# A gated recurrence in sub-blocks: gates with features on partitions, and later rounds on part of the nodes

## The chip, the cores and the metric

The kernel runs on one core of a Trainium2 chip, and all data is 32-bit floating point. The metric is the device time of one execution in microseconds (us). Engines are named as in the profile: PE (matmul), PEld (its weight loads), DVE (VectorE), ACT (ScalarE), POOL (GpSimd) and SP (SyncE, which only starts transfers).

## The reference

Four graph layers work on `x` of shape (16, 1024, 256) with a sparse weighted adjacency `adj` of shape (16, 1024, 1024). Each adds its result to `x` after a layer norm and a relu. Layers 0, 1 and 3 are dense products. Layer 2 is a recurrence over the 1024 nodes of each graph, and the change is there:

```python
def step(h, i):
    x = jnp.take(h_e, i, axis=1)
    row = jnp.take(norm_adjT, i, axis=1)
    x_par = jnp.einsum('bj,bjd->bd', row, h)
    iou = x @ W_ioux.T + b_ioux + x_par @ W_iouh.T + b_iouh
    r, z = jnp.split(iou, 2, axis=1)
    r, z = (jax.nn.sigmoid(r), jax.nn.sigmoid(z))
    hc = jnp.tanh(x @ W_coux.T + b_coux + x_par * r @ W_couh.T + b_couh)
    h_new = z * x_par + (1.0 - z) * hc
    h = jax.lax.dynamic_update_slice(h, h_new[:, None, :], (0, i, 0))
    return (h, None)
```

A node takes the weighted sum of its neighbours: the new values of those with a smaller number, the old values of the others. About one pair in 32 of different nodes is connected.

## The kernel before

**Layer 2 in blocks and rounds.** The nodes of each graph are cut into NT = 8 blocks of 128. Within a block the kernel sorts them, so that nodes which depend on each other stand as far apart as can be, and cuts the sorted block into NS = 8 sub-blocks of S = 16. One step of the loop treats sub-block (t, s) of all 16 graphs together, 256 columns of node and graph (two groups g of eight graphs with 128 each). Where no node of a sub-block depends on another of the same sub-block, one round of gates is enough. Where there is a chain of dependent nodes, the round is repeated, each time with the change in h that the round before brought: a chain of k nodes takes k rounds. The number of rounds in the program is fixed by position, and a branch on the chip runs more where the data asks for it:

```python
KS = (1, 1, 1, 1, 1, 2, 2, 4)
```

`orders` works out the sorted positions and, for every (t, s), the longest chain over the 16 graphs. It stores `need - KS[s]` in `more`. After the fixed rounds, `tc.If(n_more[0][s] > 0)` runs `one_more`, and a loop in it runs further ones.

**One round.** `x` (features on partitions) is the neighbours' sum. `round_` adds its products with `wh` to the sums `pr`, `pz` and `pc` in PSUM, which `seed_r` and `seed_zc` have filled with the parts of the gates that depend on the inputs alone (class `Gates`). `pr` has features on partitions; `pz` and `pc` have nodes on partitions. Since the product of z with the neighbours' sum needs both in one layout, `x` is turned by four PE transposes (line 815) between the products for `pr` and `pz`. ACT and DVE then make r and r*x (lines 825 and 826; in later rounds line 828 takes the difference from the round before, `drx`), PE adds the products of r*x to `pc`, and ACT and DVE make tanh and the new h (lines 842 to 844), which has nodes on partitions, as `change` (line 796) and the next sub-block's sum (line 989) need it. A later round gives PE the same amount of work as the first, and `change` besides. `ho` holds the h of the rounds before, and `change` works on the difference `dh`.

**Work that fills the gaps.** PE, DVE, ACT and POOL run in an order that is written out by hand (`tc.manual_schedule`). Between the steps of a round, `fill(weight)` puts in tasks that nothing waits for at once: sums of old values for the next block (`base_tasks`, line 615 and, to turn them, line 629), contributions of the new h to later sub-blocks (`far_tasks`, line 764) and to the next block (`next_block`, line 751; `last_tasks`, line 665). Each takes one of three PSUM buffers `pf`, and their evictions are kept in `late` until `evict()` issues them. At the end of a sub-block stand the gates' input products for the next one (lines 728 and 736; in the branch or in its else arm), then the sum at line 989, with which the next sub-block begins (line 937).

**POOL and the queues.** POOL gathers the rows of the sorted adjacency (`aj`, line 692), spreads them over graphs (`bd`, line 708, for later nodes; `ai`, line 699, for the same sub-block), copies inputs (`hs`, line 719), masks base rows (line 593), and scatters h to memory (`hs_d`, line 982). SP's queue carries the other loads.

Of the kernel before, what the change touches and what calls it, by code (L numbers as in the profile page):

```python
# [11 lines left out]
ALU = mybir.AluOpType  # L12
# [14 lines left out]
KS = (1, 1, 1, 1, 1, 2, 2, 4)  # L27
# [12 lines left out]
def gnn_stack(ctx: ExitStack, tc: tile.TileContext, a: dict, out: bass.AP):  # L40
# [65 lines left out]
    def orders(pool, psum):  # L106
# [50 lines left out]
        def rest():  # L157
# [41 lines left out]
            for s in range(NS):  # L199
                nc.vector.scalar_tensor_tensor(junk, sub, float(s), chain, op0=ALU.is_equal, op1=ALU.mult)  # L200
                nc.vector.tensor_reduce(top[:, s : s + 1], junk, AX.X, ALU.max)
            most = pool.tile([1, NS, NT], F32, name="o_most")
            for s0 in range(0, NS, 4):
                pt = psum.tile([P, 512], F32, name="pt")
                for s in range(4):
                    nc.tensor.transpose(pt[:1, s * P : (s + 1) * P], top[:, s0 + s : s0 + s + 1], ident)
                nc.vector.tensor_reduce(most[:, s0 : s0 + 4].rearrange("o s t -> o (s t)"),
                                        pt[:1].rearrange("o (q b) -> o q b", b=B), AX.X, ALU.max)
            need = pool.tile([1, NS, NT], F32, name="o_need")
            nc.vector.memset(need, 1.0)  # L210
            for k in range(1, S):
                nc.vector.scalar_tensor_tensor(need, most, 2.0 ** k, need, op0=ALU.is_ge, op1=ALU.add)
            for k in range(2):
                left = pool.tile([1, NT, NS], F32, name="o_left")
                for s in range(NS):
                    nc.vector.tensor_scalar(left[:, :, s], need[:, s], float(KS[s] + k), 0.0, op0=ALU.subtract, op1=ALU.max)
                nc.vector.tensor_copy(more[k], left.rearrange("o t s -> o (t s)"))
# [322 lines left out]

    def layer_2(shared, early):
        with ExitStack() as st:
# [9 lines left out]
            br = wp.tile([P, DC], F32, name="br")  # L552
            br2 = wp.tile([P, DC], F32, name="br2")
            with nc.allow_non_contiguous_dma(reason="biases, once"):
                nc.sync.dma_start(br, a["b_ioux"][:D].rearrange("(c p) -> p c", p=P))
                nc.sync.dma_start(br2, a["b_iouh"][:D].rearrange("(c p) -> p c", p=P))
            nc.vector.tensor_add(br, br, br2)
            bzc = wp.tile([P, 2 * D], F32, name="bzc")
            bzc2 = wp.tile([P, 2 * D], F32, name="bzc2")
            for t, io, co in ((bzc, "b_ioux", "b_coux"), (bzc2, "b_iouh", "b_couh")):  # L560
                nc.sync.dma_start(t[:, :D], bcast_row(a[io][D:], D))
                nc.sync.dma_start(t[:, D:], bcast_row(a[co], D))
            nc.vector.tensor_add(bzc, bzc, bzc2)
# [6 lines left out]
            nc.vector.tensor_mul(before, before, own[:, :, None].to_broadcast([P, GB, S]))  # L570

# [111 lines left out]
            class Sub:  # L683
# [18 lines left out]
                def behind(self):  # L702
                    n, j0 = self.n - S, (self.s + 1) * S
                    self.bd = None
                    if n > 0:
                        self.bd = big.tile([P, G2, GB, P], F32, name="bd")
# [5 lines left out]
            class Gates:  # L712

                def __init__(self, he, s):
# [4 lines left out]
                    self.gr = big.tile([P, DC, G2 * GR], F32, name="gr")  # L721
                    self.gz = big.tile([P, G2, 2 * D], F32, name="gz")
                    self.tasks = [lambda k=k: self.z(k) for k in range(G2)] + [lambda k=k: self.r(k) for k in range(DC)]

                def r(self, e):
                    pg = psum.tile([P, 2 * D], F32, name="pf", bufs=3)
                    for c in range(DC):
                        nc.tensor.matmul(pg[:, : G2 * GR], wx[:, c, e * P : (e + 1) * P], self.hs[:, c],
                                         start=c == 0, stop=c == DC - 1)
                    return lambda: nc.scalar.activation(self.gr[:, e], pg[:, : G2 * GR], AF.Identity,  # L730
                                                        bias=br[:, e : e + 1])

                def z(self, g):
                    pg = psum.tile([P, 2 * D], F32, name="pf", bufs=3)
                    for c in range(DC):
                        nc.tensor.matmul(pg, self.hs[:, c, g * GR : (g + 1) * GR], wx[:, c, D:],  # L736
                                         start=c == 0, stop=c == DC - 1)
                    return lambda: nc.vector.tensor_add(self.gz[:, g], pg, bzc)  # L738

                def seed_r(self):  # L740
                    nc.scalar.activation(pr, self.gr, AF.Copy)

                def seed_zc(self):
                    nc.scalar.activation(pc, self.gz[:, :, D:], AF.Copy)
                    nc.vector.tensor_copy(pz, self.gz[:, :, :D])
# [31 lines left out]

            pr = psum.tile([P, DC, G2 * GR], F32, name="pr")
            pz = psum.tile([P, G2, D], F32, name="pz")
            pc = psum.tile([P, G2, D], F32, name="pc")  # L780
# [10 lines left out]
            def change(dh, x, ai, fill):  # L791

                px = psum.tile([P, DC, G2 * GR], F32, name="pa")
                for g in range(G2):
                    for c in range(DC):
                        nc.tensor.matmul(px[:, c, g * GR : (g + 1) * GR], dh[:, g, c * P : (c + 1) * P], ai[:, g],
                                         start=g == 0 and c == 0, stop=True, skip_group_check=True)
                fill()
                dx = work.tile([P, DC, G2 * GR], F32, name="dx", bufs=1)
                nc.vector.tensor_copy(dx[:, 0], px[:, 0])  # L800
                nc.scalar.activation(dx[:, 1], px[:, 1], AF.Copy)
                for c in range(DC):
                    nc.vector.tensor_add(x[:, c], x[:, c], px[:, c])
                return dx

            def round_(dx, x, rx, h, fill, to):


                for e in range(DC):
                    for c in range(DC):  # L810
                        add(pr[:, e], wh[:, c, e * P : (e + 1) * P], dx[:, c])
                xr = psum.tile([P, G2, D], F32, name="pa")
                for g in range(G2):
                    for c in range(DC):
                        nc.tensor.transpose(xr[:, g, c * P : (c + 1) * P], x[:, c, g * GR : (g + 1) * GR], ident)
                for g in range(G2):
                    for c in range(DC):
                        add(pz[:, g], dx[:, c, g * GR : (g + 1) * GR], wh[:, c, D : 2 * D])
                evict()
                r = work.tile([P, DC, G2 * GR], F32, name="r")  # L820
                drx = r
                if rx is not None:
                    drx = work.tile([P, DC, G2 * GR], F32, name="drx", bufs=1)
                for e in range(DC):
                    nc.scalar.activation(r[:, e], pr[:, e], AF.Sigmoid)  # L825
                    nc.vector.tensor_mul(r[:, e], r[:, e], x[:, e])  # L826
                    if rx is not None:
                        nc.vector.tensor_sub(drx[:, e], r[:, e], rx[:, e])
                z = work.tile([P, G2, D], F32, name="z")
                nc.scalar.activation(z, pz, AF.Sigmoid)  # L830
                w = work.tile([P, G2, D], F32, name="w")
                nc.scalar.activation(w, pz, AF.Sigmoid, scale=-1.0)
                for g in range(G2):
                    for c in range(DC):
                        add(pc[:, g], drx[:, c, g * GR : (g + 1) * GR], wh[:, c, 2 * D :])
                nc.vector.tensor_mul(z, z, xr)
                if h is not None:
                    nc.vector.tensor_sub(z, z, h)
                fill()
                hc = work.tile([P, G2, D], F32, name="hc", bufs=1)  # L840
                for g in range(G2):
                    nc.scalar.activation(hc[:, g], pc[:, g], AF.Tanh)
                    nc.vector.tensor_mul(w[:, g], w[:, g], hc[:, g])
                    nc.vector.tensor_add(to[:, g], z[:, g], w[:, g])
# [3 lines left out]
            def one_more(x, rx, h, ho, ai, tasks=()):  # L848
# [6 lines left out]

                fill()
                dh = work.tile([P, G2, D], F32, name="dh", bufs=1)
                for g in range(G2):
                    nc.vector.tensor_sub(dh[:, g], h[:, g], ho[:, g])
                nc.gpsimd.tensor_copy(ho, h)  # L860
                dx = change(dh, x, ai, fill)
                r = round_(dx, x, rx, None, fill, h)
                nc.gpsimd.tensor_copy(rx, r)
# [4 lines left out]
            with tc.manual_schedule(engines={mybir.EngineType.PE, mybir.EngineType.DVE, mybir.EngineType.Activation, mybir.EngineType.Pool}):  # L868
# [7 lines left out]
                for task in gx.tasks:  # L876
                    task()()
                sub.own()
# [7 lines left out]
                for t in range(NT):  # L886
# [10 lines left out]
                    for s in range(NS):  # L897
# [6 lines left out]
                        if s == 0:  # L904
                            gx_next = Gates(he, 1)
                            todo = [(1.72, task) for task in gx_next.tasks[:2]] + [(0.86, task) for task in gx_next.tasks[2:]]
                            todo += share + behind
# [310 lines left out]
```

## Time and profile before

| | us |
|---|---|
| median of 3 runs (lowest, highest) | 4867.45 (4866.39, 4873.52) |
| span of the profiled execution | 4855.7 |
| layers 0 and 1, with the ordering | 0 to 1515 |
| layer 2 | 1515 to 3398 |
| layer 3 | 3398 to 4856 |

A line of the groups reads: line of the kernel, engine, operation, tile written <- tiles read, shape, number of instructions | busy time in us, mean duration in ns | idle time of that engine just before them, and what ended it. A line of the table by stage gives the window, its length, the busy time of PE, PEld, DVE, ACT and POOL with the number of instructions, the granted PE clock, and the share and rate of the DMA engines. A 32-bit product shows as two PE instructions, a transpose as one.

### The profile page before, as it was taken

To read this page: it belongs to the slowest core of one execution; us is meant where nothing else is said; L and a number is where in the kernel's file an instruction comes from. 1 tells how busy PE (TensorE), PEld (TensorE's weight loads), DVE (VectorE), ACT (ScalarE), POOL (GpSimd) and SP (SyncE) were. 2 spreads that over 40 slices of the span, in tenths; PEclk is the share of its full clock that TensorE was granted. 3 is DMA by queue.
4 is the path that set the end of the run, shared out by engine and by line. 5 is a ranking of instruction groups with operands and counts; after the bars stand their busy time and mean duration, and the time that the engine had idled before them with its cause. 6 is when DMAs were issued, how large, how long until landed. Compare 5 with 4: busy or idle time off the path is not lost. (4 is left out here: it accounts for less than half of the span.)

```text
span 4855.7 us, 51055 instructions
## 1 busy us (share of the span) xinstructions
PE 4521.4 (93%) x17679; PEld 2951.8 (61%) x17679; DVE 2381.2 (49%) x6366; ACT 1173.7 (24%) x2388; POOL 1602.6 (33%) x1883
## 2 busy tenths in 40 slices
PE   8897899999997999999999999988899999999999
PEld 4443445555555777777777777766455555555556
DVE  6667854455543454545454545454534344344342
ACT  1211112222212222222222222222223223223232
POOL 3223233343323333323222333232534234243231
PEclk9999999999998999999999999999899999999999
DMA  5333235555536444444443444421422231222100
GB/s 158 113 98 104 88 88 185 193 165 174 186 112 214 135 145 130 152 139 141 127 146 125 138 151 152 139 83 37 160 87 70 78 104 65 89 89 78 70 26 18
DMA packets 530494, 577.04 MB, mean 119 GB/s; under 512 B 41552, under 2 KB 438992, under 8 KB 527824
## 3 DMA queue, kind: packets, MB, share of 16 engines
q1 hardware_dynamic: 499056, 460.79, 30.1%
q0 software_dynamic: 31040, 111.44, 6.4%
q8 instruction: 189, 3.10, 0.3%
q14 instruction: 209, 1.71, 0.1%
HBM read 470.17 MB, written 116.65 MB: 121 GB/s over the span
## 5 line engine op out<-in xcount | busy, mean ns | idle before, releaser
L290 PE MATMUL pa<-at,h 128*128 128x512 f32 x1088 | 490.2, 603 | 32.8 <-DVE ag L295 32.8
L1093 PE MATMUL ph<-ag,w 128*128 128x512 f32 x1024 | 479.1, 611 | 33.9 <-DVE hh L1097 33.8
L1131 PE MATMUL po<-w,hh 128*128 128x256 f32 x2048 | 447.7, 379 | 0.0
L615 PE MATMUL pf<-hb,ab 128*128 128x256 f32 x1568 | 416.9, 385 | 24.3 <-ACT bs L602 18.8
L290 PE MATMUL pa<-at,q 128*128 128x512 f32 x960 | 424.5, 595 | 0.0
L1131 PEld LDWEIGHTS po<-w,hh 128*128 128x128 f32 x2048 | 387.8, 190 | 59.3 <-issue 7.9
L290 PEld LDWEIGHTS pa<-at,h 128*128 128x128 f32 x1088 | 207.6, 194 | 273.9 <-issue 228.1
L1093 PEld LDWEIGHTS ph<-ag,w 128*128 128x128 f32 x1024 | 179.1, 190 | 295.5 <-DVE hh L1097 151.8
L1099 POOL TENSOR_TENSOR ss<-ss,sq 128x512 f32<-128x512 f32 x224 | 302.4, 1350 | 121.8 <-ACT sq L1096 117.4
L615 PEld LDWEIGHTS pf<-hb,ab 128*128 128x128 f32 x1568 | 281.5, 192 | 75.5 <-ACT bs L602 26.1
L982 POOL DMA_INDIRECT hs_d<-h,table x128 | 129.8, 1014 | 589.0 <-DVE gz L738 420.1
L290 PEld LDWEIGHTS pa<-at,q 128*128 128x128 f32 x960 | 178.4, 190 | 215.8 <-issue 212.8
L736 PE MATMUL pf<-wx,hs 128*128 128x512 f32 x512 | 242.0, 613 | 29.2 <-POOL hs L719 21.6
L1097 DVE TENSOR_SCALAR hh<-ph,b 128x512 f32<-128x512 f32 x256 | 190.0, 746 | 154.7 <-ACT sq L1096 120.7
L1078 PE MATMUL pa<-bxt,h 128*128 128x512 f32 x512 | 228.0, 598 | 19.7 <-POOL bxt L1060 19.7
L764 PE MATMUL pf<-bd,h 128*128 128x384 f32 (+5 forms) x768 | 217.7, 371 | 28.6 <-DVE bxt L767 28.6
L826 DVE TENSOR_TENSOR r<-r,x 128x256 f32<-128x256 f32 x230 | 128.4, 581 | 225.5 <-ACT r L825 225.5
L1078 PE MATMUL pa<-at,h 128*128 128x512 f32 x512 | 228.8, 597 | 0.0
L1096 ACT ACTIVATE sq<-ph,b 128x512 f32<-128x512 f32 x224 | 153.5, 685 | 234.2 <-PE ph L1093 189.1
L1123 ACT ACTIVATE hh<-hh,rw 128x512 f32<-128x512 f32 x256 | 168.4, 712 | 138.7 <-DVE hh L1122 136.7
L1134 DVE TENSOR_TENSOR x<-x,po 128x256 f32<-128x256 f32 x120 | 50.5, 420 | 289.0 <-PE po L1131 288.9
L1078 PEld LDWEIGHTS pa<-bxt,h 128*128 128x128 f32 x512 | 97.4, 192 | 136.9 <-issue 115.3
(233 smaller groups left out, 7723.4 us busy)
## 6 DMA issues: line engine op xcount, KB each, us to landing
at<-in_adjT SPq DMA_DIRECT2D x64, 1024.0 KB
ab<-in_adj SPq DMA_DIRECT2D x128, 512.0 KB
bxt<-in_adjT SPq DMA_DIRECT2D x64, 512.0 KB
at<-in_adjT SPq DMA_DIRECT2D x64, 512.0 KB
ad<-in_adj SPq DMA_DIRECT2D x128, 128.0 KB
x_d<-x POOLq DMA_DIRECT2D x16, 1024.0 KB, 5.4
he_d<-h POOLq DMA_DIRECT2D x16, 1024.0 KB, 9.3
heT_d<-hT POOLq DMA_DIRECT2D x16, 1024.0 KB, 4.2
```

What stands on the lines that cost most here:

```text
L290: nc.tensor.matmul(pa, h[:, mt, c * P : (c + 1) * P], at[n0 // 512][:, mt], start=mt == 0, stop=mt == NT - 1)
L615: nc.tensor.matmul(pb, ab[:, jts[k]], hb[:, jts[k]], start=k == 0, stop=k == len(jts) - 1)
L736: nc.tensor.matmul(pg, self.hs[:, c, g * GR : (g + 1) * GR], wx[:, c, D:], start=c == 0, stop=c == DC - 1)
L764: nc.tensor.matmul(pf, h[:, g, c * P : (c + 1) * P], bd[:, g, b4 : b4 + 4, S : S + far], start=True, stop=True)
L982: nc.gpsimd.indirect_dma_start(out=hs_d[t][g][:, :], out_offset=row(1, g, t, s), in_=h[:, g], in_offset=None)
L1078: nc.tensor.matmul(pa, h[b][:, mt, c * P : (c + 1) * P], at[b][n0 // NH][:, mt], start=mt == 0, stop=mt == NT - 1)
L1093: nc.tensor.matmul(ph, w1[:, c, k * P : (k + 1) * P], ag[:, c, n0 : n0 + NH], start=c == 0, stop=c == DC - 1)
L1096: nc.scalar.activation(sq, ph, AF.Square, bias=b1[:, k : k + 1])
L1097: nc.vector.tensor_scalar(hh[:, k], ph, b1[:, k : k + 1], None, op0=ALU.add)
L1099: nc.gpsimd.tensor_tensor(ss, ss, sq, ALU.add)
L1123: nc.scalar.activation(hh[:, k], hh[:, k], AF.Silu, scale=rw[:, k : k + 1])
L1131: nc.tensor.matmul(po, hh[:, c, k * P : (k + 1) * P], w2[:, c], start=c == 0, stop=c == HC - 1)
```

## The change

All gates of layer 2 now have features on partitions; h comes out as `hT` with features on partitions and is turned to nodes on partitions by four PE transposes and two ACT copies (`turned`). The transposes of `x` are gone. Rounds after the first work only on the nodes from a position `cut` on: `CUTS` gives it for each later round. KS of the last position goes from 4 to 5. `orders` looks also for chains among nodes ahead of a cut, and where it finds one sends all of the sub-block's later rounds to the branch. `one_more` no longer works with differences: it seeds the three sums again from the inputs and does a full round. POOL prepares `bd` of the next sub-block one sub-block ahead (three buffers), behind the first h of the current one: the small copies into `tick` hold it back until then. The gates' biases are loaded with features on partitions.

```diff
-KS = (1, 1, 1, 1, 1, 2, 2, 4)
+KS = (1, 1, 1, 1, 1, 2, 2, 5)
+CUTS = {5: (8,), 6: (8,), 7: (4, 4, 12, 12)}
...
+            for s, cuts in CUTS.items():
+                for k, cut in enumerate(cuts):
+                    if cut in cuts[:k]:
+                        continue
+                    nc.vector.tensor_scalar(junk, pos, float(s * S + cut), None, op0=ALU.is_lt)
+                    nc.vector.scalar_tensor_tensor(junk, sub, float(s), junk, op0=ALU.is_equal, op1=ALU.mult)
+                    nc.vector.scalar_tensor_tensor(junk, chain, 2.0 ** (k + 1), junk, op0=ALU.is_ge, op1=ALU.mult)
+                    nc.vector.tensor_reduce(found, junk, AX.X, ALU.max)
+                    nc.vector.tensor_tensor(early[:, s : s + 1], early[:, s : s + 1], found, ALU.max)
...
+            for s in range(NS):
+                nc.vector.scalar_tensor_tensor(need[:, s], again[:, s], float(KS[s] - 1), need[:, s], op0=ALU.mult, op1=ALU.add)
...
-                        self.bd = big.tile([P, G2, GB, P], F32, name="bd")
+                        self.bd = big.tile([P, G2, GB, P], F32, name="bd", bufs=3)
...
-                    self.tasks = [lambda k=k: self.z(k) for k in range(G2)] + [lambda k=k: self.r(k) for k in range(DC)]
+                    self.g = big.tile([P, 3, DC, G2 * GR], F32, name="gates")
+                    self.tasks = [lambda q=q: self.gate(q) for q in (1, 2, 0)]
...
-                xr = psum.tile([P, G2, D], F32, name="pa")
-                for g in range(G2):
-                    for c in range(DC):
-                        nc.tensor.transpose(xr[:, g, c * P : (c + 1) * P], x[:, c, g * GR : (g + 1) * GR], ident)
-                for g in range(G2):
-                    for c in range(DC):
-                        add(pz[:, g], dx[:, c, g * GR : (g + 1) * GR], wh[:, c, D : 2 * D])
...
+                for q, pg in ((0, pr), (1, pz)):
+                    for e in range(DC):
+                        for c in range(DC):
+                            add(from_(pg[:, e], cut), wh[:, c, q * D + e * P : q * D + (e + 1) * P], dx[:, c])
...
+            def turned(hT, fill, to):
+
+                ph = psum.tile([P, DC, G2, P], F32, name="pa")
+                for e in range(DC):
+                    for g in range(G2):
+                        nc.tensor.transpose(ph[:, e, g], hT[:, e, g * GR : (g + 1) * GR], ident)
+                fill()
+                for e in range(DC):
+                    nc.scalar.activation(to[:, :, e * P : (e + 1) * P], ph[:, e], AF.Copy)
+                evict()
...
-                dx = change(dh, x, ai, fill)
-                r = round_(dx, x, rx, None, fill, h)
-                nc.gpsimd.tensor_copy(rx, r)
+                px = x_change(h, ai, 0)
+                fill()
+                gx.seed_r()
+                gx.seed_zc()
...
+                round_(xm, xm, None, 0, None, fill, hT)
+                turned(hT, fill, h)
...
-                        sub.behind()
...
+                        rx = round_(x, x, None, 0, None, rest_if(False, 1.3), hT)
...
+                            nc.gpsimd.tensor_copy(tick, rx[:, DC - 1, :1])
...
+                        turned(hT, rest_if(K == 1, 0.5), dh)
                         if sub_next:
+                            nc.gpsimd.tensor_copy(tick, dh[:, G2 - 1, D - 1 :])
+                            sub_next.behind()
                             sub_next.own()
...
+                            if last:
+                                rx = round_(dx, xs, rx, cut, None, rest_if(False, 1.3), hT)
+                                turned(hT, rest_if(True, 0.5), h)
+                            else:
+                                rx = round_(dx, xs, rx, cut, hT, rest_if(False, 1.3), changes[cut])
                                 dh = work.tile([P, G2, D], F32, name="dh", bufs=1)
+                                turned(changes[cut], rest_if(False, 0.5), dh)
+                                nc.gpsimd.tensor_tensor(from_(hT, cut), from_(hT, cut), from_(changes[cut], cut), ALU.add)
```

## The prediction

> **What bounds the kernel now.** I read the page first (busy shares), then the table by stage, then sub-blocks of the recurrence one by one, then the groups by shape, then the order of time inside one sub-block.
>
> ```profile
> PE 4521.4 (93%) x17679; PEld 2951.8 (61%) x17679; DVE 2381.2 (49%) x6366; ACT 1173.7 (24%) x2388; POOL 1602.6 (33%) x1883
> ```
> The table by stage, layer 2 alone (window, us, then busy time of PE, weight loads, DVE, ACT, POOL):
> ```profile
> 1515.00:3398.00 1883.00, 1753.82 (x8538) 1400.47 (x8536) 922.87 (x2165) 486.06 (x1134) 578.84 (x818) 0.99 0.41 131
> ```
> PE is busy 93% of it: only 129 us can be won by shorter waits, the rest by less PE work. Six windows, each one sub-block (t,s) = (2,2), (3,2), (2,5), (2,7), (3,7), (7,7):
>
> ```profile
> 2033.00:2059.00 26.00, 24.29 (x110) 18.19 (x110) 10.77 (x25) 5.68 (x14) 9.43 (x13) 1.00 0.48 149
> 2261.00:2294.50 33.50, 31.11 (x146) 23.99 (x146) 16.40 (x40) 8.93 (x22) 9.25 (x13) 1.00 0.36 113
> 2109.00:2137.00 28.00, 27.67 (x146) 23.07 (x145) 14.38 (x37) 8.21 (x20) 7.82 (x13) 1.00 0.37 120
> 2166.00:2213.30 47.30, 46.05 (x234) 38.72 (x232) 25.37 (x61) 14.65 (x37) 10.54 (x17) 1.00 0.41 132
> 2419.80:2475.60 55.80, 53.17 (x271) 44.42 (x269) 31.11 (x75) 17.76 (x45) 9.88 (x17) 1.00 0.33 106
> 3343.00:3398.00 55.00, 40.72 (x172) 32.94 (x172) 26.82 (x62) 14.27 (x36) 4.74 (x5) 0.87 0.16 54
> ```
> A trip through the branch costs 33.5 - 26.0 = 7.5 us at s=2 and 55.8 - 47.3 = 8.5 us at s=7. PE idles 1.7 us in a one-round sub-block, 0.3 at s=5, 1.3 at s=7. The groups:
>
> ```profile
> L863 POOL COPY r<-r 128x512 f32<-128x512 f32 x11 | 6.7, 613 | 81.4 <-DVE drx L828 81.4
> L826 DVE TENSOR_TENSOR r<-r,x 128x256 f32<-128x256 f32 x230 | 128.4, 581 | 225.5 <-ACT r L825 225.5
> L843 DVE TENSOR_TENSOR w<-w,hc 128x256 f32<-128x256 f32 x230 | 97.0, 422 | 144.9 <-ACT hc L842 144.2
> L783 PE MATMUL pc<-wh,r 128*128 128x256 f32 x512 | 125.3, 385 | 12.3 <-DVE r L826 12.2
> L764 PE MATMUL pf<-bd,h 128*128 128x192 f32 x128 | 32.1, 339 | 6.0 <-DVE bxt L767 6.0
> L764 PE MATMUL pf<-bd,h 128*128 128x128 f32 x128 | 24.7, 280 | 0.0
> L764 PE MATMUL pf<-bd,h 128*128 128x64 f32 x128 | 22.2, 260 | 5.3 <-DVE bxt L767 5.3
> ```
> L863 stands in the branch alone: eleven trips. A product shows as two instructions; L764 runs in pairs, so the pitch is a pair's busy time less one duration: 2x0.251-0.339 = 0.163 us at 192 columns, 0.106 at 128, 0.087 at 64. And the end of a round at s=7:
>
> ```profile
> 2435.17 1.89 PE L783 MATMUL pc<-wh,drx 128*128 128x256 f32 x8
> ...
> 2437.12 1.89 PE L615 MATMUL pf<-hb,ab 128*128 128x256 f32 x8
> 2437.16 0.66 ACT L842 ACTIVATE hc<-pc 128x256 f32<-128x256 f32 x2 [0.70 <-PE pc L783]
> ...
> 2438.83 0.42 DVE L844 TENSOR_TENSOR dh<-z,w 128x256 f32<-128x256 f32 x1
> 2438.85 1.18 PE L796 MATMUL pa<-ai,dh 128*128 128x128 f32 x8
> ```
> Eight instructions of 256 columns take 1.89, four (L615 elsewhere) 1.03: pitch 0.215. The new h is complete 2.2 us after pc; queued base work (L615) covers that.
>
> **What the skill says.** TensorE: Matmul & The Clock Gate, § Architectural detail: ACT and DVE are strict FIFO, PE only draws weight loads ahead; so a transpose waiting for h stops all PE work behind it, as L764 behind an unread pf buffer does here. Same page, § LDWEIGHTS: 128 weight columns take P/1.2 = 107 ns, a floor for narrow matmuls; the trace is a little below (0.087 at 64 columns), and I use the trace. Same page, Part 1: an idle stretch of about 3.4 us halves the PE clock; the (7,7) window, at 0.87, agrees. SBUF — State Buffer, § Who interferes with whom: a DVE instruction with two SBUF inputs waits for a GpSimd instruction that reads SBUF. Agrees: r*x and w*hc have one shape, but r*x ran while POOL built bd (581 against 422 ns).
>
> **The change part by part.** Sums are against the profiled span, 4855.7; the three timed runs have median 4867.45, and I carry the difference over.
>
> *Trips.* The inputs are fixed, and the ordering (bins, positions, chains) can be stepped through on them: chains exceed KS in 11 sub-blocks, as L863 shows: five at s=7 (t=0,3,4,6,7), all of five links, six at s=2 to 4. With KS[7]=5 the five go; no node ahead of a cut has a long chain, so `again` is zero everywhere. Left: six trips.
>
> *s=5 and s=6.* Round two has 128 columns: 24x(0.215-0.106) = 2.6 us of PE less. But its r chain becomes the limit: 0.2 from pr's last column, ACT 0.27 (by the line through L825, 381 ns at 256, and L830, 597 at 512), DVE 2x0.28 (L767 at 128 columns: 281 ns), 1.03 us in all against 8x0.106 = 0.85 of pz; with the second half of drx behind it, some 0.6 us of wait. The turn of h after round one (four transposes 0.43, 0.2, two ACT copies 0.66) adds 1.3 us behind a fill of about 10% and 0.5 to 1 us shows. Net -1.1 (bounds -2.3, +1) x14, -1 for t=7: -16 us.
>
> *s=7.* Before: three later rounds at 24x0.215+0.43+0.86 (change) = 6.45. After: two at 24x0.163+1.29 = 5.2, two at 24x0.087+1.29 = 3.4: PE -2.2. Added: four turns in fills of 4%, 0.5 each; r chains 0.8; and bd of the next block (L708 at 1024: 2x1.91 us on POOL, moved behind the first dh) collides with r*x of round two, 1.0. Net about +2 (bounds -1, +6) x8 = +16; five trips x-8.5 = -42.5. Sum -26.
>
> *One-round sub-blocks.* PE work is the same: gates 24x0.215 = 5.2 against 8x0.43+8x0.215 = 5.2; four transposes move from x to h. Post-pc fill is 46% of the todo work, 4 to 6 us for t<7, over the 2.2 us until h; behind them on PE stand the last fill and the gates (5.2), under which ACT's copies to h lie; behind those on ACT stands only a bs of the base, which the next fill needs. So nothing, bounds -0.3 and +0.8 each, -12 to +32 over 40. At t=7 fill is 1 to 2 us: +2. In POOL's queue `tick` holds bd and ai (up to 4.7 us) until h; behind them stand only the scatter to hs_d, masks and the next gather, used a sub-block later. With bd off the r chain, the 12.2 us before pc shrink: -8 (bounds 0, -12).
>
> *The six trips left.* Without h-ho, drx and the POOL copies; with three seeds (ACT 0.60+0.58, DVE 0.69, under the first gate task, 1.7) and a turn: PE 0.86+5.2+0.43 = 6.5 as before. Nothing; bounds -1, +2 each.
>
> *Start and ordering.* bd goes ahead of ai and the second hs on POOL: its 3.8 us delay the first gates (today 1513.8): +4. Biases come as single elements on SP's queue ahead of he: 0 to +3, in that. `orders` gains 4x5 DVE operations of about 0.3 us and eight PE transposes queued behind them: +3 (0 to 7).
>
> Sum: -16 -26 +2 -8 +4 +3 = -41 us. 4867 - 41 = 4826.
>
> **The rivals.** *The turn shows everywhere (slower).* If hT comes late (ACT's bs copies stand ahead of hc when a turn of base falls in that fill, up to 0.9 us) PE stops at the transposes in all 64 sub-blocks and six trips. At 1.1 us each, +77: 4903. It decides above 0.6 us each. For it: 1.3 us of new latency in each round, no fill at t=7; against it: 4 to 6 us of fill in 35 of 64. *More gain.* The 1.7 us of one-round idle come mostly from L764 waiting for a pf buffer whose eviction DVE has behind h; splitting the fill evicts earlier. Half of it back over 40: -28 more, 4798. *A wash.* Narrow rounds are all latency: s=5 and 6 gain nothing (+16), s=7 costs +4 (+16): 4858. *It doesn't do what it says*, cuts failing into the branch: the inputs exclude it.
>
> **How the numbers follow.** About 0.2% (10 us) can be told from no change. Forecast 55% (4800 to 4855), more gain 18%, a wash 11%, turn shows 16%. The wash lies at the edge and is split, 3% faster and 8% same: faster 0.76, same 0.08, slower 0.16. The range 4790 to 4882 takes in more gain, the wash, and the low end of the slower case.
>
> **What would show it.** Right: no L863-like trips at s=7 (about 49 us in each block), s=5 near 27, one-round windows near 26 and 24, r*x near 422 ns. Wrong: PE idle before the transposes of hT over 1 us a sub-block, s=7 without a trip above 53, or layers 0 and 1 longer by over 10.

## The result, and the profile after

The changed kernel is slower: 4911.49 us, median of 4 runs (4903.53 to 4916.15), against 4868.41 for the kernel before; the ratio is 1.0085, 95% interval 1.0068 to 1.0103. I had forecast 4826. The profiled spans are 4908.1 and 4855.7, so 52.4 us are to be explained in them; that is 9 more than the 43 of the medians, because the profiled execution of the kernel before was some 10 us shorter than its median.

Less PE work, and still a longer span. The page's busy shares of the changed kernel:

```profile
PE 4510.6 (92%) x18307; PEld 3022.5 (62%) x18307; DVE 2290.3 (47%) x6408; ACT 1213.9 (25%) x2651; POOL 1586.5 (32%) x1947
```

The table by stage for layer 2, which lasts 1928.9 us now (window, us, then busy time of PE, weight loads, DVE, ACT, POOL, granted PE clock, DMA share, GB/s):

```profile
1522.20:3451.10 1928.90, 1737.22 (x9152) 1467.28 (x9152) 822.31 (x2175) 524.45 (x1397) 557.99 (x884) 0.98 0.42 127
```

PE's busy time fell from 1754 to 1737 us, but its idle time rose from 129 to 192. The layer starts 7.5 us later (1522.2 against 1514.7). The same six windows as in the prediction, sub-blocks (2,2), (3,2), (2,5), (2,7), (3,7) and (7,7):

```profile
2053.70:2081.00 27.30, 24.60 (x118) 19.65 (x117) 10.78 (x25) 6.23 (x15) 8.91 (x15) 1.00 0.44 131
2294.60:2330.40 35.80, 32.81 (x153) 26.36 (x153) 15.19 (x35) 9.97 (x25) 8.90 (x15) 0.95 0.32 95
2134.80:2163.00 28.20, 26.23 (x155) 22.84 (x154) 11.98 (x36) 8.36 (x23) 7.60 (x15) 1.00 0.41 118
2190.60:2243.90 53.30, 48.47 (x278) 40.69 (x276) 23.84 (x74) 16.60 (x52) 12.80 (x19) 1.00 0.37 112
2454.00:2508.30 54.30, 48.75 (x278) 40.77 (x276) 24.12 (x73) 17.20 (x53) 13.51 (x20) 1.00 0.36 110
3397.50:3451.10 53.60, 38.90 (x172) 33.56 (x172) 19.25 (x61) 13.04 (x44) 4.48 (x7) 0.72 0.15 46
```

The trips at s=7 are gone: (2,7) and (3,7) are alike. But a one-round sub-block went from 26.0 to 27.3 us, and a block at s=7 without a trip from 47.3 to 53.3. Added up over t from the start of each sub-block in the trace, after less before, us:

| s=0 | s=1 | s=2 | s=3 | s=4 | s=5 | s=6 | s=7 | start |
|---|---|---|---|---|---|---|---|---|
| +20 | -2 | +14 | +6 | +17 | -1 | -13 | +5 | +7.5 |

The sub-blocks s=0 to 4, where I had expected next to nothing, cost 55 us, more than the whole difference. The groups of PE in layer 2 of the changed kernel, with shapes kept apart, name the waits:

```profile
L749 PE MATMUL pf<-hs,wx 128*128 128x256 f32 x1512 | 349.2, 387 | 15.8 <-POOL hs L740 15.8
L1037 PE MATMUL pa<-bd,h 128*128 128x128 f32 x448 | 64.6, 287 | 52.7 <-ACT gates L757 41.6 <-ACTq L1016 5.9 <-DVEq L1014 4.6
L870 PE MATMUL pa<-ident,hT 128*128 128x128 f32 x376 | 61.7, 279 | 14.4 <-DVE hT L861 13.3 <-DVE w L860 1.1
L827 PE MATMUL pa<-ai,dh 128*128 128x32 f32 x128 | 18.9, 294 | 8.1 <-ACT dh L873 8.1
L870 PE MATMUL pa<-ident,change 128*128 128x128 f32 x96 | 18.5, 291 | 9.2 <-DVE change L861 8.2 <-DVE w L860 1.0
L827 PE MATMUL pa<-ai,dh 128*128 128x96 f32 x128 | 18.3, 286 | 7.1 <-ACT dh L873 5.8 <-issue 1.3
L771 PE MATMUL pnx<-bd,h 128*128 128x128 f32 x448 | 60.1, 277 | 6.0 <-ACT gates L757 5.2 <-issue 0.8
```

In the kernel before, the sum (L989) and the products that read hs (L736) read:

```profile
L989 PE MATMUL pa<-bd,h 128*128 128x128 f32 x448 | 60.1, 277 | 9.4 <-DVEq L966 4.7 <-DVEq L968 4.1 <-PEq L966 0.7
L736 PE MATMUL pf<-wx,hs 128*128 128x512 f32 x502 | 233.6, 606 | 15.5 <-POOL hs L719 7.9 <-DVE bxt L767 3.7 <-ACT bs L602 3.6
```

L1037 is the sum of h with which a sub-block hands over to the next (L989 before). PE waits 41.6 us there, and the releaser is not the turned h (L873) but L757, ACT's eviction of the r gates: 0.99 us at the end of each of the 42 sub-blocks s=1 to 6 without a trip. L771 is the sum's counterpart at the end of s=7. The end of sub-block (2,4) in the changed kernel, in order of time:

```profile
2125.73 0.66 ACT L873 ACTIVATE h<-pa 128x256 f32<-128x256 f32 x2 [6.74 <-PE pa L870]
...
2127.29 5.34 PE L749 MATMUL pf<-hs,wx 128*128 128x256 f32 x24
...
2132.73 0.84 ACT L757 ACTIVATE gates<-pf,bias 128x256 f32<-128x256 f32 x2 [4.70 <-PE pf L749]
...
2133.63 1.16 PE L1037 MATMUL pa<-bd,h 128*128 128x128 f32 x8 [0.99 <-ACT gates L757]
2133.85 1.04 POOL L1030 DMA_INDIRECT hs_d<-h,table  x1 [4.75 <-ACT gates L757]
```

h is complete at 2126.4 us, 7 us before the sum that reads it. Between them lies the branch, with the gates (L749) in both its arms. Behind the branch the sum and POOL's scatter of h start only when ACT has done the last thing it does in the arm. It is h that they wait for and not the PSUM bank `pa`, which ACT reads last and into which L1037 writes: the scatter does not touch the bank, and L771 writes to `pnx`, which ACT never reads, yet both wait for L757. The same place in the kernel before, where DVE wrote h:

```profile
2106.04 1.89 PE L728 MATMUL pf<-hs,wx 128*128 128x256 f32 x8
...
2106.24 0.69 DVE L738 TENSOR_TENSOR gz<-pf,bzc 128x512 f32<-128x512 f32 x1 [0.95 <-PE pf L736]
2107.17 0.47 ACT L730 ACTIVATE gr<-pf,br 128x256 f32<-128x256 f32 x1 [3.82 <-PE pf L728]
2107.22 0.97 POOL L982 DMA_INDIRECT hs_d<-h,table  x1 [0.61 <-DVE gz L738]
...
2107.77 1.05 PE L989 MATMUL pa<-bd,h 128*128 128x128 f32 x8
2107.97 0.48 ACT L730 ACTIVATE gr<-pf,br 128x256 f32<-128x256 f32 x1 [0.33 <-PE pf L728]
```

There too this scatter, the second of two, starts behind DVE's last eviction of the arm (L738, ending 2106.93). That end lies ahead of the end of PE's last gate products, so PE does not wait; ACT's last eviction begins at 2107.97, after the sum has begun. Here h is written in two halves, one for each group of graphs, and the first scatter, which reads the first half, started at 2105.57, behind DVE's last eviction but one. It looks as if the readers wait for a count of the writer's instructions; no run shows more of the reason.

At s=0 the wait goes through POOL. The scatter (L1030) is late, so is the copy of hs behind it in POOL's queue, and the gates of (t,1), which read hs, are the first work of s=0. Sub-block (2,0) in the order of time, changed kernel:

```profile
1999.83 0.84 ACT L757 ACTIVATE gates<-pf,bias 128x256 f32<-128x256 f32 x2 [5.18 <-PE pf L749]
...
2000.94 1.04 POOL L1030 DMA_INDIRECT hs_d<-h,table  x1 [15.12 <-ACT gates L757]
...
2003.28 0.75 POOL L740 COPY hs<-he 128x256 f32<-128x256 f32 x2
...
2003.74 7.13 PE L749 MATMUL pf<-hs,wx 128*128 128x256 f32 x24 [2.23 <-POOL hs L740]
```

The 24 instructions of these products take 7.13 us, against 5.34 in (2,4): the idle 2.23 us are followed by a stretch at half clock. The table by stage, for 6 us that begin within these products, shows a granted clock of 0.81 with PE busy throughout:

```profile
2006.00:2012.00 6.00, 6.00 (x24) 5.09 (x23) 1.38 (x2) 0.84 (x2) 1.02 (x3) 0.81 1.12 384
```

This wait for hs is not all new. The kernel before has 7.9 us of it in the line of L736 above, 1.9 to 2.4 us at s=0 behind each of the four blocks that end with a trip, and under 0.1 behind the other three; the changed kernel has it behind all seven.

The theory of the experiments: **the arm's end**. h counts as written, behind the branch, only when the engine that wrote it has reached the end of its work in the arm. The rival: **the turn itself**, the longer way from pc to h (transposes, copies), costs time in each sub-block, as my slower rival had it. A second question is why a block at s=7 takes 53 us and not 49.

### The profile page after: what moved, and what is told of

Same layout as the page of the kernel before. It is cut to its first block, busy times and chain, and to the rows that moved or that the text cites. A ratio compares the mean times of both kernels' runs of the same rounds, so it can differ in the third digit from the quotient of the medians.

```text
span 4908.1 us, 52731 instructions
## 1 busy us (share of the span) xinstructions
PE 4510.6 (92%) x18307; PEld 3022.5 (62%) x18307; DVE 2290.3 (47%) x6408; ACT 1213.9 (25%) x2651; POOL 1586.5 (32%) x1947
## 5 line engine op out<-in xcount | busy, mean ns | idle before, releaser
L637 PE MATMUL pf<-hb,ab 128*128 128x256 f32 x1568 | 435.1, 390 | 22.1 <-ACT bs L624 18.8
L749 PE MATMUL pf<-hs,wx 128*128 128x256 f32 x1536 | 358.3, 390 | 30.0 <-POOL hs L740 30.0
L749 PEld LDWEIGHTS pf<-hs,wx 128*128 128x128 f32 x1536 | 297.5, 196 | 74.8 <-POOL hs L740 33.1
L1030 POOL DMA_INDIRECT hs_d<-h,table x128 | 129.4, 1011 | 490.6 <-ACT gates L757 386.9
L754 DVE TENSOR_TENSOR gates<-pf,bias 128x512 f32<-128x512 f32 x128 | 88.4, 691 | 231.6 <-PE pf L749 231.6
```

Of the source, the lines that this page charges most:

```text
L637: nc.tensor.matmul(pb, ab[:, jts[k]], hb[:, jts[k]], start=k == 0, stop=k == len(jts) - 1)
L749: nc.tensor.matmul(pg[:, e], wx[:, c, q * D + e * P : q * D + (e + 1) * P], self.hs[:, c], start=c == 0, stop=c == DC - 1)
L1030: nc.gpsimd.indirect_dma_start(out=hs_d[t][g][:, :], out_offset=row(1, g, t, s), in_=h[:, g], in_offset=None)
```

## The experiments

All times are medians; ratios are to the kernel before, whose median beside these runs is 4869. Labels name the edit.

**Which engine writes h** (e1_turn_on_dve):

```diff
-                    nc.scalar.activation(to[:, :, e * P : (e + 1) * P], ph[:, e], AF.Copy)
+                    nc.vector.tensor_copy(to[:, :, e * P : (e + 1) * P], ph[:, e])
```

> The changed kernel with the two copies that end a turn of h on DVE instead of ACT; the gates' order stays. Theory (the arms' end): since ACT writes h, the sum that opens the next sub-block waits, behind the branch, for the last thing that ACT does in the arm, the eviction of the r gates, which comes after the last gate product. With DVE writing h it waits for DVE, whose last work in the arm lies two thirds of the gates earlier. So the 0.99 us before the near sum (sub-blocks 1 to 6) and the 0.75 us at s=7 go, and at s=0 the scatter and the hs copies come about 1 us earlier: 50 to 62 us less, 4849 to 4861. Rival (the turn itself is too long): two copies of 0.42 on DVE are no shorter than two of 0.38 on ACT, so the time stays at 4911 within 10. Rival (PE clock): nothing changes.

Measured: 4855.63, ratio 0.9969 (0.9961 to 0.9977). This is the range of the theory. The turn is no shorter, its copies have only changed engine (420 ns each on DVE, 382 on ACT), and 56 us are gone.

**In which order the arm's work comes** (e2_r_gates_first): the r gates, which ACT evicts, first instead of last.

```diff
-                    self.tasks = [lambda q=q: self.gate(q) for q in (1, 2, 0)]
+                    self.tasks = [lambda q=q: self.gate(q) for q in (0, 1, 2)]
```

> The changed kernel with the gates in the order r, z, c: ACT's eviction comes first in the arm, DVE's last. Theory (the arms' end) in its narrow form, ACT alone: the wait before the near sum goes, 4850 to 4861. In its wide form (behind the branch PE waits for the last work of every engine that wrote h or touched the bank in either arm, DVE too since one_more reads the bank there): the wait changes hands, DVE's eviction of 0.69 us against ACT's 0.84, and the time falls by 10 or less, 4900 to 4911. Rival (the turn is too long): no change.

Measured: 4833.97, ratio 0.9925 (0.9908 to 0.9942), 77 us less than the changed kernel; the turn is untouched. More than expected, because s=0 gained too (29 us over its seven later sub-blocks, while s=1 to s=7 together gained 46). The groups of layer 2, this run:

```profile
L749 PE MATMUL pf<-hs,wx 128*128 128x256 f32 x1512 | 341.5, 381 | 2.9 <-POOL hs L740 2.2 <-issue 0.7
L1037 PE MATMUL pa<-bd,h 128*128 128x128 f32 x448 | 63.2, 284 | 15.4 <-DVEq L1016 5.6 <-DVEq L1014 4.8 <-ACTq L1014 0.7
```

No wait for ACT's gates is left before the sum, and none for DVE's has come in its place, as the wide form would have it; for hs it is 2.2 instead of 15.8 us. Sub-block (2,0) in the order of time:

```profile
1985.19 0.84 ACT L757 ACTIVATE gates<-pf,bias 128x256 f32<-128x256 f32 x2 [1.73 <-PE pf L749]
...
1986.31 1.04 POOL L1030 DMA_INDIRECT hs_d<-h,table  x1 [11.67 <-ACT gates L757]
...
1988.64 0.75 POOL L740 COPY hs<-he 128x256 f32<-128x256 f32 x2
...
1989.28 5.35 PE L749 MATMUL pf<-hs,wx 128*128 128x256 f32 x24
```

The scatter still waits for L757, but L757 now comes early; the 24 instructions take 5.35 us. Layer 2 fell from 1928.9 to 1853.6 us: PE's idle time by 55 and its busy time, for the same number of instructions, by 20. Most of the 20 is the half clock: by the trace's record of the granted clock PE was busy at half speed for 88 us of layer 2 in the changed kernel and for 54 in this run (36 in the kernel before), and half of that difference is 17 us.

**The same in the kernel before** (b1_z_gates_last): there DVE writes h and evicts the z and candidate gates, so these are put last.

```diff
-                    self.tasks = [lambda k=k: self.z(k) for k in range(G2)] + [lambda k=k: self.r(k) for k in range(DC)]
+                    self.tasks = [lambda k=k: self.r(k) for k in range(DC)] + [lambda k=k: self.z(k) for k in range(G2)]
...
-                            todo = [(1.72, task) for task in gx_next.tasks[:2]] + [(0.86, task) for task in gx_next.tasks[2:]]
+                            todo = [(0.86, task) for task in gx_next.tasks[:2]] + [(1.72, task) for task in gx_next.tasks[2:]]
```

> The kernel before with the gates in the order r, then z and c, nothing else. There DVE writes h, and DVE evicts z and c. Theory (the arms' end): the near sum now waits for DVE's eviction after the last gate product, about 0.9 us in sub-blocks 1 to 7 and the scatter before s=0 with it: 45 to 60 us more, 4913 to 4928, the loss of the change without any of the change. Rival (turn, narrow rounds or clock cause the loss): the order of the gates is indifferent, 4868 within 10.

Measured: 4924.5, ratio 1.0121 (1.0103 to 1.0139). An order of gates alone, with no turn of h anywhere, costs the kernel before 55 us, as the theory said, and PE's idle time ahead of its sum (9.4 us before) has the name that the theory gives:

```profile
L989 PE MATMUL pa<-bd,h 128*128 128x128 f32 x448 | 71.2, 287 | 34.6 <-DVE gz L738 23.7 <-DVEq L968 5.6 <-DVEq L966 4.7
```

**Both edits at once** (e6_r_first_turn_on_dve): r gates first as in e2, copies on DVE as in e1. Each alone is a gain; by the theory they undo each other, since DVE then evicts last and writes h.

> The changed kernel with the r gates first and, besides, the copies of the turned h on DVE. Both edits alone made it faster (by 56 and by 77 us). Arms' end: with r first, DVE evicts the gates last (c), so h written by DVE ties the next sub-block's sum to the end of the arm again: slower than with r first alone by 15 to 30 us, 4849 to 4865, with a wait for DVE's gates before the sum. Rival (each edit is a gain of its own, by less ACT work or an earlier turn): 4775 to 4825, both gains together.

Measured: 4904.27, ratio 1.0072 (1.0053 to 1.009). Seventy us slower than e2, and beyond the range that I had given: as at s=0 in the changed kernel, the wait for hs came back too, which I had not counted. The groups of layer 2:

```profile
L749 PE MATMUL pf<-hs,wx 128*128 128x256 f32 x1512 | 350.0, 388 | 18.0 <-POOL hs L740 18.0
L1037 PE MATMUL pa<-bd,h 128*128 128x128 f32 x448 | 63.3, 284 | 47.9 <-DVE gates L754 36.8 <-DVEq L1016 5.6 <-DVEq L1014 4.8
```

The four kernels make a square, in which each edit helps or hurts according to the other:

| us | ACT evicts last (r gates last) | DVE evicts last (r gates first) |
|---|---|---|
| ACT writes h | 4911.5 | 4834.0 |
| DVE writes h | 4855.6 | 4904.3 |

As the cause of the loss the turn falls with this: it is in all four. So does a gain of its own for either edit, by less work on ACT for instance.

**Rounds at full width** (e3_full_rounds): the changed kernel with all later rounds over all nodes.

```diff
-CUTS = {5: (8,), 6: (8,), 7: (4, 4, 12, 12)}
+CUTS = {5: (0,), 6: (0,), 7: (0, 0, 0, 0)}
...
-            changes = {cut: wp.tile([P, DC, G2 * GR], F32, name=f"change{cut}") for cut in (4, 12)}
+            changes = {cut: wp.tile([P, DC, G2 * GR], F32, name=f"change{cut}") for cut in (0,)}
```

> The changed kernel with every cut at 0: later rounds take all 256 columns. Theory (narrow rounds gain, as the forecast had it): s=5 and s=6 lose 1.1 to 2.6 us each (18 to 40 in all) and s=7 about 6 to 8 us a block (48 to 64): 4977 to 5015. Rival (narrow rounds are all latency, and cause the loss): within 10 of 4911, or less.

Measured: 5004.9, ratio 1.0277 (1.0258 to 1.0296), in the range of the theory: narrowing alone is worth 93 us.

**The kernel before with five rounds** (b2_five_rounds):

```diff
-KS = (1, 1, 1, 1, 1, 2, 2, 4)
+KS = (1, 1, 1, 1, 1, 2, 2, 5)
```

> The kernel before with five rounds at s=7 instead of four and nothing else: the five trips at s=7 go, eight full-width rounds come. My prediction's step (a trip at s=7 costs 8.5 us): a full round costs about the same as a trip, so +8 x 8.5 - 5 x 8.5 = +25 us: 4894 (4884 to 4904). Rival (the branch itself, its jump and its empty fills, is the dear part, a round inside the block is cheaper by over 3 us): 4870 or less.

Measured: 4877.51, ratio 1.0017 (1.0008 to 1.0026): 8 us and not 25, between the two ranges. The block (2,7) takes 54.6 us, so the fifth round costs 7.3 us where a trip costs 8.5, and 8 x 7.3 - 5 x 8.5 = +16, as in the traces (s=7 in sum 438 against 422). The trace of the kernel before is of an execution some 10 us shorter than its median, so 16 there and 8 in the medians do not contradict each other. These two runs split the price of a block at s=7. The block (2,7) in the table by stage, first the kernel before with five rounds, then the changed kernel with full rounds:

```profile
2167.30:2221.90 54.60, 53.88 (x271) 44.26 (x269) 31.02 (x73) 17.80 (x44) 11.34 (x18) 1.00 0.36 116
```
```profile
2214.30:2276.20 61.90, 56.24 (x278) 44.61 (x276) 31.33 (x74) 20.43 (x52) 14.21 (x19) 1.00 0.31 97
```

Rounds and width are equal; layout, turn and POOL's order differ. They cost 7.3 us a block, of which 2.4 are PE's busy time and 4.9 its idle time (0.9 of it the arm's end, at L771). No run tells layout, turn and POOL's order apart. Narrowing takes 8.6 us a block off (61.9 to 53.3).

**Four rounds at s=7, r gates first** (e5_r_first_four_rounds), e2 with:

```diff
-KS = (1, 1, 1, 1, 1, 2, 2, 5)
-CUTS = {5: (8,), 6: (8,), 7: (4, 4, 12, 12)}
+KS = (1, 1, 1, 1, 1, 2, 2, 4)
+CUTS = {5: (8,), 6: (8,), 7: (4, 4, 12)}
```

> The changed kernel with the r gates first (4834 us) and with four rounds at s=7 instead of five, so that the five trips at s=7 come back: what did the fifth round cost, and what did the trips? Reading of the traces: the fifth round takes 8.5 us in each of eight blocks (a no-trip block 53 -> about 44.5: -68 us), a trip with a turn 8.5 to 9.5 us (+45): about 4811 us (4800 to 4825). My prediction's own figures (a round of 64 columns for about 5 us, a trip for 8.5): -40 + 42, no difference, 4836. If a trip with three seeds and a turn costs over 13 us, this run is slower than 4834.

Measured: 4818.54, ratio 0.989 (0.987 to 0.991): the fastest kernel of this study, 93 us below the changed one and about 50 below the one before. Its blocks (2,7), without a trip, and (3,7), with one:

```profile
2159.00:2204.80 45.80, 43.97 (x248) 37.60 (x247) 23.44 (x60) 15.11 (x45) 13.43 (x20) 1.00 0.45 140
2403.80:2457.70 53.90, 50.72 (x280) 42.64 (x279) 27.77 (x70) 19.14 (x55) 12.61 (x19) 1.00 0.37 114
```

A trip costs 8.1 us. The fifth round costs 53.0 (e2) - 45.8 = 7.2 us, although it has a quarter of the columns and the full-width one of b2 costs 7.3. So -7.2 x 8 + 8.1 x 5 = -17, and -15 was measured.

**The start of the layer** (e7_four_own_first), e5 with ai and the masks ahead of bd at the start:

```diff
-                sub.behind()
                 sub.own()
+                sub.behind()
```

> As the run with the r gates first and four rounds, but at the start of the layer the near matrices are built behind ai and the first masks, as in the kernel before: only the layer's first 8 us are touched. My prediction put +4 on this at the start (3.8 us of POOL ahead of the second sub-block's hs): so 2 to 4 us less than that run; nothing in between the rest.

Measured: 4824.84 (4817.88 to 4829.77), ratio 0.9909 (0.9887 to 0.993), against e5's 4812.53 to 4825.2: the spreads overlap, so nothing can be told. In the traces the layer's first sub-block takes 17.2 us in this run and 18.5 in e5, but it takes 17.0 in the changed kernel, which starts as e5 does. So the 2 to 4 us that I had said are not shown.

## Why the prediction was wrong

**The step that failed** is that of the one-round sub-blocks: behind the transposes stand "the last fill and the gates (5.2), under which ACT's copies to h lie", "So nothing, bounds -0.3 and +0.8 each". The copies do lie there: the transposes of hT wait 14.4 us in all, but in one-round sub-blocks only in the six with a trip, 0.3 us each, and h is ready 7 us early. But I asked only when h is ready. The reader stands behind a branch, and there it is released by the last work of h's writer in the arm. The change moved the writer from DVE to ACT, whose last work hangs on PE's last gate product. Price: 0.99 us of PE at the end of each sub-block s=1 to 6 without a trip (41.6 us), 5.2 at s=7, and for hs at s=0 about half of 15.8, since the kernel before had 7.9. The forecast also had no term for the clock, though it had named the half clock: PE's busy time at half speed rose from 36 to 88 us, which costs half of the difference, 26. Layer 2 as a whole grew by 46 us: 62 more of idle time and 26 of half clock, less 43 of PE work that is gone. e2 takes 77 us back, more than was lost, in part since it also removes waits for hs that the kernel before has. I had named the scatter in POOL's queue and called it "used a sub-block later"; I had not asked what it waits for now, nor that hs for the next gates stands behind it at s=0.

**The slower rival** came near in number (4903) by luck: it put the wait before the transposes, at 1.1 us in each sub-block, and one-round sub-blocks without a trip have none there. e2 keeps the turn and is 0.75% faster than the kernel before. Only at s=7 does the turn show, as follows.

**s=7** was mis-sized. Said: about 49 us in each block, in sum -26 with the five trips. Measured: 53.0, and +5 in sum. That the trips go was right, and their price too (8.5; e5 has 8.1). Wrong was the narrow round. A round over 64 columns in (2,7) of the changed kernel, pr to pr (the order of time):

```profile
2222.91 1.00 PE L802 MATMUL pr<-dx,wh 128*128 128x64 f32 x8
...
2223.75 1.06 PE L802 MATMUL pz<-dx,wh 128*128 128x64 f32 x8
...
2225.86 1.95 PE L637 MATMUL pf<-hb,ab 128*128 128x256 f32 x8
...
2229.05 1.08 PE L827 MATMUL pa<-ai,dh 128*128 128x32 f32 x8 [0.38 <-ACT dh L873]
...
2230.65 1.00 PE L802 MATMUL pr<-dx,wh 128*128 128x64 f32 x8
```

From the start of pr to that of pz eight instructions take 0.84 us, a pitch of 0.105 and not the 0.087 that I read out of pairs; at s=5, with 128 columns, the same eight take 0.89. The Trainium skill, TensorE: Matmul & The Clock Gate, § LDWEIGHTS, gives 107 ns for 128 weight columns; the trace agrees here, and I had set it aside. From start to start of its pieces the round takes PE 0.84 (pr), 0.99 (pz), 1.12 (pc, which meets the r chain), 0.44 (turn) and 0.91 (change), 4.3 us where I had put 3.4; a round of 192 columns, in the same way (the second of (2,7) in e5), 5.8 where I had put 5.2. So PE's own time rose, from 46.05 to 48.47 us in (2,7), where I had said 2.2 less. Its idle time rose by 3.6, from 1.25 to 4.83, near the 3.8 that turns, r chains and bd had been given (2 + 0.8 + 1.0), but only by luck, since the parts differ. In (2,7) of the changed kernel PE waits 1.5 us at the transposes and 1.7 at the products of dh, 3.2 for four turns where I had put 2; 0.5 at the products of drx, where r chains and bd had 1.8; and 0.9 at L771, the arm's end, which I had not counted. Waits of 1.2 us of the kernel before are nearly gone. Of the 4 us by which a block is longer than said, some 3 are thus the narrow rounds' own PE time, mis-sized by 0.6 us in two rounds and 0.9 in two; the rest is not told apart.

**s=5 and s=6**: -14 against -16 said, which is luck: it holds 0.99 us of arm's end in each, and without it (e2: 215 and 211 us, against 224 and 232) it is -30. So the r chains and turns cost less than I had put, and the gain lay nearer the bound of -2.3.

**Held**: r*x takes 422 ns in the first round, as I had expected with bd moved off it. PE waits 4.3 instead of 12.3 us for it:

```profile
L844 DVE TENSOR_TENSOR r<-r,x 128x256 f32<-128x256 f32 x128 | 48.8, 422 | 139.5 <-ACT r L843 112.1 <-issue 27.4
```

This is the -8 of the sum, and it agrees again with the Trainium skill, SBUF — State Buffer, § Who interferes with whom (581 ns on average before). The start and the ordering were said to cost 7 and cost 7.5, which one pair of traces cannot confirm: layer 2 starts at 1514.8 to 1523.9 us in the seven traces with the new start, and at 1510.2 to 1514.7 in the three with the old one. The six trips left were priced at nothing; the one in (3,2) costs 35.8 - 27.3 = 8.5 instead of 7.5 us, with a clock of 0.95.

The sum from the traces: +55 for s=0 to 4 (said -6, with t=7 and the wait for r*x), -14 for s=5 and 6 (said -16), +5 for s=7 (said -26 with its trips), +7.5 for the start (said +7): +53, against 52.4 in the spans. t=7 is in these rows. Left open: in e2 the sub-blocks s=2 to 4 are still 14 us above the kernel before, while s=0 and 1 are 18 below it.

## What to carry to other kernels

When a value is written ahead of a branch and read behind it, ask not only when it is ready but what its writer does last inside the arms. In this program two edits won the time back: putting that engine's work first in the arm (e2), or letting the engine that ends first write the value (e1). Together they lost it again (e6), so moving a copy to another engine was a gain or a loss of over 1% by that alone. And a narrower round saved PE time only down to 128 columns: eight instructions took 0.84 us at 64 columns and 0.89 at 128.

## What was not expected of the hardware

PE's half clock came without an idle stretch of 3.4 us, the window that the Trainium skill, TensorE: Matmul & The Clock Gate, Part 1, gives for it. In (7,7) of the kernel before, which the prediction took as agreeing, PE's longest idle stretch is 2.7 us. Ahead of the gates of (2,0) in the changed kernel it idled for 2.23 us; the next 3.4 us ran at half speed, and the 24 instructions took 7.13 instead of 5.35 us. The table by stage for these two windows:

```profile
2001.40:2004.80 3.40, 1.17 (x6) 0.95 (x6) 1.36 (x3) 0.60 (x1) 2.93 (x5) 1.00 0.33 80
2004.80:2008.20 3.40, 3.40 (x10) 2.69 (x9) 0.69 (x1) 0.00 (x0) 1.91 (x4) 0.51 0.91 301
```

All changes of the granted clock in this trace lie on one grid of 3.41 us, the length of the skill's window. In layer 2 of the changed kernel the clock went from full to half 20 times; in 19 of them PE had been idle for 1.71 to 2.63 us of the window just before, often in several stretches. Of 518 windows that were followed by full speed, two had more than 1.6 us of idle time. So in this kernel idle time of about half a window, added up, was enough, and a wait of 0.99 us could cost more than it lasted where other waits stood in the same window. In e2 55 us of idle time and 20 us of busy time went together.
